# Four layers of a graph network on one core: row factors in smaller pieces, records gathered by fours, a ring of five PSUM banks

## The chip, the cores and the metric

The kernel runs on one core of a Trainium2 chip, as one program. A core has four compute engines with a queue each: PE (TensorE, with weight loads shown apart as PEld), DVE (VectorE), ACT (ScalarE) and POOL (GpSimd); SP issues DMAs. Matrices' sums are formed in PSUM, in 8 banks of 128 x 512 float32; all other data of the core lie in SBUF.[...] The metric is the device time of one launch in microseconds (us), as the median of several runs; the traces each hold one profiled execution.

## The reference

There are 8192 nodes with 32 features, `x`, and 262144 edges sorted by destination, so 32 a node in the mean. Four layers follow on each other; each adds its sum over the edges to x and normalizes the rows:

```python
edge_index = jnp.stack([src, dst])
x = _layernorm(x + _L0_gnn_ref(x, L0_gnn_weight, src, dst, edge_type_64), axis=-1)
x = _layernorm(x + _L1_gnn_ref(x, edge_index, edge_weight), axis=-1)
x = _layernorm(x + _L2_gnn_ref(x, edge_index), axis=-1)
x = _layernorm(x + _L3_gnn_ref(x, edge_index, edge_attr_4, edge_attr_32, L3_gnn_W1, ...), axis=-1)
```

Layer 0 multiplies `x[src]` with one of 64 matrices of 32 x 32, chosen by the edge's type, and sums over the edges of each destination. Layer 1 sums `x[src] * edge_weight`, layer 2 sums `x[src]`. Layer 3 makes for each edge a vector of 256 weights, `w = relu(ea32 @ W1 + b1) @ W2 + b2`, read as four 8 x 8 matrices, and combines them with the gathered row and the edge's four numbers `edge_sh`:

```python
m0 = ALPHA * (einsum('ei,eio->eo', s_e * sh0[:, None], w_000)
              + C110 * einsum('eim,em,eio->eo', v_e, sh1, w_110))
m1 = ALPHA * (einsum('ei,em,eio->eom', s_e, sh1, w_011)
              + einsum('eim,eio->eom', v_e * sh0[:, None, None], w_101))
```

where `s_e` are the first 8 features of `x[src]` and `v_e` the other 24 as 8 x 3. `m0` and `m1` are summed over each destination's edges, and a small product of x itself is added.

## The kernel before

Edges are worked in tiles of 128 (one edge per partition); 2048 tiles make 256 groups of 8. A sum over destinations is a matmul of a one-hot matrix (128 edges x 128 places of a moving window of nodes; `one_hot`, L505) with the tile's values; the groups' windows are brought together later by shifted matmuls (`windows`, L495). The order of the work is the order in which this code issues it to each engine's queue. `X.after(mark)` makes engine X wait for a mark, `X.mark(ins)` makes one. Helpers: `own` marks an operation and makes its engine wait for it, `now(X)` is X's newest mark, and a `Landing` counts the arrivals of DMAs. All indirect gathers (128 rows by 128 indices) are issued by POOL in one place, `indirect`, so they carry L383 in the profile.

**Table, from the start.** For every node and edge type the product is made once: 64 steps, each four matmuls (L404), two evictions of 128 x 1024 (L410) and one store of 1 MB into `ytab` (L412, by SP) from a ring of `NY` = 5 buffers. Beside it the generator `beginnings()` runs, one piece (up to the next `yield`) per step: it counts edges per node by one-hot matmuls (L321, L325, L326), takes prefix sums (from L346), then gathers 64 records of 768 bytes a partition (`begun["rec"]`), and checks. The 64 gathers are issued in one piece. While the generator has pieces left (`busy`), ACT makes both evictions of a step, afterwards ACT and DVE one each. The gathers of layer 0 wait for all stores of the table.

**Layer 0.** `slots` turns the gathered records about (PE transposes, ACT's evictions L537). Then for each group: eight row gathers from `ytab`, 12 groups ahead, in two halves by `fetch_rows`, where the first half waits for the mark of that group's aggregation on PE and the second for PE's newest mark; the split into three bf16 parts on DVE (`parts`, L619 to L624); the one-hot (L505); eight matmuls (L657) into bank 0 or 1, which change over every four groups; and, from group 8 on, `matrices`, which builds the adjacency matrices of layers 1 and 2 for the coming layers: one-hots on DVE (L557, L559, L562), then four units of eight matmuls each (L571) into one of two bank pairs, 3/4 and 5/6, two evictions by ACT of 128 x 512 a unit (L575, L576, one of each kind of matrix), and stores of 1 MB and 0.5 MB by SP (L580, L581). After every four groups `bank_out` reduces the aggregate bank, and eight times in the layer `windows` accumulates in bank 2 and `normalize` follows.

**Layers 1 and 2** load these matrices back and multiply (L730, L733).

**Layer 3.** First the z-stage adds the small product: 16 times a transpose (PE L852), an eviction (ACT L854), a matmul (PE L856) and an add on DVE. Then a loop over 512 quads of four tiles: `hidden` makes two quads' hidden vectors (PE L883, ACT L891); PE makes the 256 weights of four tiles (L907) in one of two bank pairs and marks `w`; `fetch_rows` issues the four gathers of the quad `AHEAD` = 12 further on, which wait for the `w` of the quad just made; PE aggregates the quad four back (L916), which waits for its `v`; DVE multiplies weights with factors (L944, L947, three L951), forms the one-hot (L505), and its mark `v` frees the weights' banks too. L931 and L936 end the quad before. The factors, products of the gathered row with `edge_sh`, are made for 32 tiles (8 quads) at once, two quads before they are needed: `factors`, L825 to L836.

Of the kernel before, what the change touches and what calls it, by code (L numbers as in the profile page):

```python
# [21 lines left out]
P = 128  # L22
# [123 lines left out]
def raw_layers(tc, x, a, w0, w1, b1, w2, si, m, bad):  # L146
# [34 lines left out]
    def now(f):  # L181
        return (f.sem, f.n)
# [100 lines left out]
    def beginnings():  # L283
# [72 lines left out]
        im = own(V, V.e.tensor_scalar(idx, idx, RG.bit_length() - 1, None, op0=OP.arith_shift_right))  # L356

        G.after(im)
        r_ld = Landing(tc, "ld_rec")
        for k in range(64):  # L360
            begun["rec"] = r_ld.add(indirect(rg[:, k].rearrange("p s f -> p (s f)"), a["rec"], idx[:, k:k + 1]))
# [4 lines left out]
        V.after(src_in, row_in)  # L366
        begun["row"] = own(V, V.e.scalar_tensor_tensor(row, src, float(R), row, op0=OP.mult, op1=OP.add))
# [173 lines left out]

    oh_used = [None, None]
    bank_free = [None, None]
# [4 lines left out]
    def matrices(i):  # L548

        b, pp, k0 = i % 2, i // 2, 16 * (i % 2)  # L550
        WB = 8
        if i % WB == 0:
            n = min(WB * 16, CB * 16 - i * 16)
            V.after(now(V))
            own(V, V.e.tensor_copy(w_ps[:, 0:n], meta_w.rearrange("p n k -> p (n k)")[:, i * 16:i * 16 + n]))
        V.after(oh_used[b])
        own(V, V.e.tensor_tensor(oh_k[:, b, :, 0, :], iota[:, None, 0:64].to_broadcast([P, 16, 64]),  # L557
                                 meta_k[:, pp, k0:k0 + 16, None].to_broadcast([P, 16, 64]), op=OP.is_equal))
        V.e.tensor_tensor(oh_l[:, b], iota[:, None, :].to_broadcast([P, 16, P]),  # L559
                          meta_l[:, pp, k0:k0 + 16, None].to_broadcast([P, 16, P]), op=OP.is_equal)  # L560
        wo = (i % WB) * 16
        vm = V.mark(V.e.tensor_tensor(oh_k[:, b, :, 1, :], oh_k[:, b, :, 0, :],  # L562
                                      w_ps[:, wo:wo + 16, None].to_broadcast([P, 16, 64]), op=OP.mult))
        PE.after(vm)
        for q in range(4):
            bk = 3 + 2 * (units[0] % 2)
            PE.after(bank_free[units[0] % 2])
            for j in range(4):
                for h in range(2):
                    hs_ = slice(64 * h, 64 * h + 64)  # L570
                    ins = PE.e.matmul(bank[:, bk + h, :].rearrange("p (c s j) -> p c s j", s=64, j=4)[:, :, :, j],  # L571
                                      oh_l[hs_, b, 4 * q + j, :], oh_k[hs_, b, 4 * q + j], start=True, stop=True)
            pm = PE.mark(ins)
            A.after(pm, st_ld[b].mark() if q == 0 and st_ld[b].n else None)
            A.e.activation(st_c[:, b, q], bank[:, bk:bk + 2, 0:256], AF.Copy)  # L575
            bank_free[units[0] % 2] = am = A.mark(A.e.activation(st_a[:, b, q], bank[:, bk:bk + 2, 256:512], AF.Copy))  # L576
            units[0] += 1
        oh_used[b] = pm
        S.after(am)
        st_ld[b].add(S.e.dma_start(amat[:, 2048 * i:2048 * (i + 1)], st_a[:, b].rearrange("p u h c -> p (u h c)")))  # L580
        st_ld[b].add(S.e.dma_start(cmat[:, 2048 * i:2048 * (i + 1)], st_c[:, b].rearrange("p u h c -> p (u h c)")))  # L581
# [6 lines left out]
    acc_free = [None]  # L588
# [50 lines left out]
    for g in range(GG + 2):  # L639
        if g >= 2 and (g - 2) % per == per - 1:  # L640
            vm = bank_out((g - 2) // per)
            while done < NB // LC and ready(done) <= g - 1:
                pm = windows(done, bank[:, 2, 0:LC * D], (acc_free[0], vm))
                acc_free[0] = normalize(0, done, bank[:, 2, 0:LC * D], pm, x_a, x_b)
# [119 lines left out]
    vs = cut(WT, 8, 3)  # L764
    a1 = cut(WT, 8)
# [42 lines left out]
    AHEAD = 12  # L808
    rows = {}

    def fetch_rows(q):

        if q < NQ:
            G.after(quad.get(q - AHEAD, {}).get("w"))
            rows[q // 8] = gathers(xtab, src, q // 8, q % 8 * 4, 4)

    def factors(s):

        k, landed = rows[s]
        b = batch[s]  # L820
        b["xg"] = k
        shv = sh[:, s % 3]
        u = s % 2
        V.after(b["s"])
        sm = V.mark(V.e.tensor_scalar(shv, shv, ALPHA, None, op0=OP.mult))  # L825
        V.after(*landed, sm)
        xv = xg[:, k]
        v = xv[:, :, 8:].rearrange("p t (i m) -> p t i m", m=3)
        vmk = V.mark(V.e.tensor_tensor(vs, v, shv[:, :, None, 1:4].to_broadcast([P, WT, 8, 3]), op=OP.mult))
        V.e.tensor_tensor(a0[:, u, :, 0:8], xv[:, :, 0:8], shv[:, :, 0:1].to_broadcast([P, WT, 8]), op=OP.mult)  # L830
        V.e.tensor_tensor(vm[:, u].rearrange("p t m i -> p t i m"), v,
                          shv[:, :, None, 0:1].to_broadcast([P, WT, 8, 3]), op=OP.mult)
# [3 lines left out]
        b["f"] = V.mark(V.e.tensor_scalar(a0[:, u, :, 8:16], a1, float(C110), None, op0=OP.mult))  # L836
# [62 lines left out]
    for q in range(NQ + LAG3 + 2):  # L899
# [21 lines left out]
        if q % 8 == 6 and q // 8 + 1 < NS:  # L921
            s = q // 8 + 1
            factors(s)
        V.after(prev)
        if q < NQ:
            V.after(batch[q // 8]["f"])
# [11 lines left out]
        if q < NQ:  # L938
# [3 lines left out]
            pq = p[:, q % NP]  # L942
            V.after(quad[q]["w"])
# [6 lines left out]
            for mm in range(3):  # L950
                V.e.tensor_tensor(pq[:, :, 128 + 64 * mm:192 + 64 * mm].rearrange("p t (o i) -> p t o i", i=8),  # L951
                                  wp[:, :, 192:256].rearrange("p t (o i) -> p t o i", i=8),
                                  vm[:, u, qs, mm, None, :].to_broadcast([P, 4, 8, 8]), op=OP.mult)
            ins = one_hot(oh[:, q % NO], 4 * q, 4)
# [501 lines left out]
```

## Time and profile before

| what | value |
|---|---|
| median of 3 runs | 7668.28 us (7660.74 to 7670.0) |
| the profiled execution | 7583.78 us |
| its span, first to last instruction | 7581.8 us |
| mean granted TensorE clock | 0.794 |
| table: to the first row gather of layer 0 | 271.4 us |
| layer 0: last row gather | 3432.6 us |
| layer 3: first row gather | 4522.6 us |
| HBM read, written | 521 MB, 472 MB |

The page's second part shows the stages by tenths of busy time in slices of 190 us (DMA is the busy share of the core's 16 DMA engines):

```profile
PE   5326665556555665654544867889989988888998
...
DVE  3336676677676767764000005666666667666676
...
POOL 3466565656566666650000016666666666666663
...
DMA  8416655556555555668999971111111111111111
```

The first slice and a half are the table, slices 2 to 18 mostly layer 0, 19 to 23 layers 1 and 2 (DMA at 6 to 9), the rest layer 3. In a row of a group or a timeline, "DMA_INDIRECT f_arena<-fytab,f_row" is a row gather of layer 0, `f_arena<-fxtab,f_src` one of layer 3; "remote" and "another core or an unknown queue" are waits for which the profile names no releaser. A wait for several semaphores is put down to the one that came last.

### The profile page before, as it was taken

The page shows a single profiled execution, that of the slowest core. Times are in us where ns is not written, and L with a number is a line of the kernel's source. Part 1 is how long each engine was busy: PE and PEld are TensorE (multiplying, and loading weights), DVE is VectorE, ACT ScalarE, POOL GpSimd, SP SyncE. Part 2 cuts the span into 40 slices and gives each one's busy share as a digit, 9 for nine tenths or more (in the row PEclk, how much of TensorE's full clock was granted, in tenths as well). Part 3 has the DMA queues.
Part 4 walks back from the last instruction along what each step waited for, and adds up shares of the span by engine and source line. Part 5 has one row for each costly group of instructions (what it writes and reads, how often), then busy time and mean ns, then how long its engine had stood idle before and what let it go on. Part 6 is the DMA issues. An engine that isn't in the chain of part 4 may idle for free.

```text
span 7581.8 us, 85791 instructions
## 1 busy us (share of the span) xinstructions
PE 5254.6 (69%) x34036; PEld 3717.5 (49%) x34036; DVE 4352.7 (57%) x8312; ACT 1629.6 (21%) x2812; POOL 3996.6 (53%) x4174
## 2 busy tenths in 40 slices
PE   5326665556555665654544867889989988888998
PEld 2115555555555555553222434555555555555555
DVE  3336676677676767764000005666666667666676
ACT  3213333333333333332000001111111111111111
POOL 3466565656566666650000016666666666666663
PEclk7557677777777777777777877999998999899989
DMA  8416655556555555668999971111111111111111
GB/s 285 149 36 145 144 150 139 145 144 152 145 145 145 144 151 138 152 142 279 428 431 428 386 289 18 28 23 25 24 24 24 24 24 24 24 24 24 25 24 20
DMA packets 290731, 999.29 MB, mean 132 GB/s; under 512 B 99021, under 2 KB 175886, under 8 KB 250638
## 3 DMA queue, kind: packets, MB, share of 16 engines
q1 hardware_dynamic: 155742, 916.89, 32.2%
q0 software_dynamic: 134144, 73.67, 12.2%
q8 instruction: 269, 4.41, 0.2%
q10 hardware_dynamic: 432, 3.15, 0.1%
q14 instruction: 144, 1.18, 0.1%
HBM read 521.39 MB, written 471.99 MB: 131 GB/s over the span
## 4 chain that ended last, share of the span: by engine, by line
PE 55%; another core or an unknown queue 11%; DMA 11%; issue 9%; DVE 8%; ACT 5%; POOL 0%; SPq 0%; DVEq 0%; ACTq 0%; POOLq 0%
PE bank L571 18%; PE bank L916 14%; PE bank L907 11%; DMA f_arena<-famat 7%; PE bank L657 3%; PE bank L883 3%; DMA f_arena<-fcmat 3%; ACT f_arena L576 3%; PE bank L730 2%; PE bank L733 2%; ACT f_arena L575 2%; DVE f_arena L951 1%; DVE f_arena L505 1%; PE bank L495 1%
## 5 line engine op out<-in xcount | busy, mean ns | idle before, releaser
L383 POOL DMA_INDIRECT f_arena<-fxtab,f_src x2048 | 1967.3, 961 | 2099.2 <-DVE f_arena L787 1089.0
L383 POOL DMA_INDIRECT f_arena<-fytab,f_row x2048 | 1962.0, 958 | 1280.5 <-issue 548.2
L571 PE MATMUL bank<-f_arena 64*128 64x128 f32 x16384 | 1566.7, 365 | 963.4 <-ACT f_arena L576 682.8
L571 PEld LDWEIGHTS bank<-f_arena 64*128 64x128 f32 x16384 | 1463.3, 272 | 1100.6 <-issue 938.7
L916 PE MATMUL bank<-f_arena 128*128 128x344 f32 x4096 | 1420.3, 489 | 65.4 <-issue 63.7
L907 PE MATMUL bank<-f_arena 65*128 65x256 f32 x4096 | 1075.3, 405 | 176.2 <-issue 161.0
L916 PEld LDWEIGHTS bank<-f_arena 128*128 128x128 f32 x4096 | 842.8, 207 | 509.3 <-issue 217.5
L907 PEld LDWEIGHTS bank<-f_arena 65*128 65x128 f32 x4096 | 785.2, 198 | 559.3 <-issue 361.0
L575 ACT ACTIVATE f_arena<-bank 128x512 bf16<-128x512 f32 x1024 | 613.0, 599 | 1925.4 <-PE bank L571 816.8
L891 ACT ACTIVATE f_arena<-bank,f_arena 64x512 f32<-64x512 f32 x512 | 351.3, 686 | 2500.1 <-remote 1001.6
L557 DVE TENSOR_TENSOR f_arena<-bank,f_arena 128x1024 f32<-128x1024 f32 x256 | 313.3, 1224 | 759.8 <-PE bank L657 440.4
L505 DVE TENSOR_TENSOR f_arena<-bank,f_rel 128x512 f32<-128x512 f32 (+1 forms) x768 | 660.9, 861 | 139.9 <-ACT f_arena L537 127.7
L944 DVE TENSOR_TENSOR f_arena<-bank,f_arena 128x256 f32<-128x256 f32 x512 | 214.7, 419 | 845.0 <-PE bank L907 324.4
L576 ACT ACTIVATE f_arena<-bank 128x512 f32<-128x512 f32 x1024 | 611.7, 597 | 0.0
L559 DVE TENSOR_TENSOR f_arena<-bank,f_arena 128x2048 f32<-128x2048 f32 x256 | 586.6, 2291 | 8.8
L951 DVE TENSOR_TENSOR f_arena<-bank,f_arena 128x256 f32<-128x256 f32 x1536 | 552.0, 416 | 0.0
L730 PE MATMUL bank<-f_arena,f_x_b 128*32 128x256 f32 x4096 | 293.2, 457 | 344.9 <-DMA f_arena<-famat 344.9
L657 PE MATMUL bank<-f_arena 128*128 128x96 bf16 x2048 | 216.7, 222 | 357.7 <-issue 215.5
L730 PEld LDWEIGHTS bank<-f_arena,f_x_b 128*32 128x32 f32 x4096 | 145.1, 131 | 481.8 <-DMA f_arena<-famat 318.0
L454 DVE TENSOR_TENSOR f_lnf<-bank,f_x_b 128x256 f32<-128x256 f32 x8 | 3.4, 425 | 615.0 <-PE bank L710 615.0
L947 DVE TENSOR_TENSOR f_arena<-bank,f_arena 128x512 f32<-128x512 f32 x512 | 348.8, 681 | 0.0
L657 PEld LDWEIGHTS bank<-f_arena 128*128 128x128 bf16 x2048 | 122.0, 104 | 404.5 <-issue 260.2
(133 smaller groups left out, 3532.6 us busy)
## 6 DMA issues: line engine op xcount, KB each, us to landing
famat<-f_arena SPq DMA_DIRECT2D x256, 1024.0 KB
fcmat<-f_arena SPq DMA_DIRECT2D x256, 512.0 KB
fytab<-f_arena SPq DMA_DIRECT2D x64, 1024.0 KB
f_arena<-fytab,f_row POOLq DMA_INDIRECT x2048
f_arena<-fxtab,f_src POOLq DMA_INDIRECT x2048
f_arena<-laid_ea SPq DMA_DIRECT2D x64, 512.0 KB
f_arena<-laid_ea SPq DMA_DIRECT2D x64, 64.0 KB
f_arena<-laid_xT ACTq DMA_DIRECT2D x1, 1024.0 KB, 8.9
```

What stands on the lines that cost most here:

```text
L383: return G.e.indirect_dma_start(out=dest, out_offset=None, in_=table, in_offset=bass.IndirectOffsetOnAxis(ap=ix, axis=0))
L505: return V.e.tensor_tensor(o, iota[:, None, :].to_broadcast([P, n, P]), rel[:, t:t + n, None].to_broadcast([P, n, P]), op=OP.is_equal)
L559: V.e.tensor_tensor(oh_l[:, b], iota[:, None, :].to_broadcast([P, 16, P]), meta_l[:, pp, k0:k0 + 16, None].to_broadcast([P, 16, P]), op=OP ...
L571: ins = PE.e.matmul(bank[:, bk + h, :].rearrange("p (c s j) -> p c s j", s=64, j=4)[:, :, :, j], oh_l[hs_, b, 4 * q + j, :], oh_k[hs_, b, ...
L575: A.e.activation(st_c[:, b, q], bank[:, bk:bk + 2, 0:256], AF.Copy)
L576: bank_free[units[0] % 2] = am = A.mark(A.e.activation(st_a[:, b, q], bank[:, bk:bk + 2, 256:512], AF.Copy))
L657: ins = PE.e.matmul(bank[:, bk, 3 * c * D:3 * (c + 1) * D], oh[:, h, t, :], xp[:, g % 4, t].rearrange("p c f -> p (c f)"), start=(t == 0), ...
L730: ins = PE.e.matmul(bank[q * D:(q + 1) * D, b, 0:256].rearrange("p (u h j) -> p u h j", h=2, j=4), x_b[:, s, :], mv[:, s], start=(s < 4), ...
L891: quad[q + h] = dict(h=A.mark(A.e.activation(hs[0:64, (q + h) % 4], bank[64 * h:64 * h + 64, 2, :], AF.Relu, bias=b1_s[64 * h:64 * h + 64])))
L907: ins = PE.e.matmul(wp[:, t, :], hs[0:65, q % 4, t * P:(t + 1) * P], w2_s[0:65], start=True, stop=True)
L916: ins = PE.e.matmul(bank[:, g % 2, 0:MW], oh[:, c % NO, t, :], p[:, c % NP, t, :], start=(c % 2 == 0 and t == 0), stop=(c % 2 == 1 and t = ...
L951: V.e.tensor_tensor(pq[:, :, 128 + 64 * mm:192 + 64 * mm].rearrange("p t (o i) -> p t o i", i=8), wp[:, :, 192:256].rearrange("p t (o i) - ...
```

## The change

Three edits in one step, and two moves of single operations on DVE.

- **Records by fours.** After each four of the 64 record gathers the generator gives way twice to the table's steps (once from the 48th on), and POOL waits for PE's newest mark before it goes on. The 64 gathers take 26 further pieces, so `busy` holds until step 60 of 64 in place of 34. The operation that makes `row` (L367) goes ahead of the gathers.
- **Ring of five banks.** The units of `matrices` take the banks 2 to 6 in turn, two a unit; each half of a unit is evicted by itself, so there are four evictions of 128 x 256 a unit, and each bank is given back by itself. A unit's first matmul waits for its two banks. Bank 2 is now in the ring, so the windows of layer 0 are accumulated in the aggregate bank that `bank_out` has just reduced, and that bank is free after `normalize` has read it.
- **Factors by 8 tiles.** `factors(r)` makes the factors of 8 tiles, the two quads after the present two, every second quad; only the scaling of `edge_sh` (L825) stays at 32 tiles. The scratch tiles `vs` and `a1` are cut to 8 tiles, so each call waits for the last one. `AHEAD` of layer 3 goes from 12 to 8.
- **One-hot first.** In a quad of layer 3 the one-hot stands ahead of the wait for `w`, and the last of the three L951 bears the mark `v`.

```diff
@@ -354,17 +354,21 @@
         own(V, V.e.tensor_scalar(idx, pre[:, 1 - f, :], small[:, 7:8], None, op0=OP.add))
         own(V, V.e.tensor_scalar(idx2, idx, RG - 1, None, op0=OP.bitwise_and))
         im = own(V, V.e.tensor_scalar(idx, idx, RG.bit_length() - 1, None, op0=OP.arith_shift_right))
+        V.after(src_in, row_in)
+        begun["row"] = own(V, V.e.scalar_tensor_tensor(row, src, float(R), row, op0=OP.mult, op1=OP.add))
 
         G.after(im)
         r_ld = Landing(tc, "ld_rec")
         for k in range(64):
+            if k % 4 == 0 and k:
+                for _ in range(2 if k < 48 else 1):
+                    yield
+                G.after(now(PE))
             begun["rec"] = r_ld.add(indirect(rg[:, k].rearrange("p s f -> p (s f)"), a["rec"], idx[:, k:k + 1]))
         yield
 
         own(V, V.e.tensor_tensor(pre[:, f, :], idx2, deg, op=OP.add))
         own(V, V.e.tensor_reduce(ok[:, 3:4], pre[:, f, :], AX.X, OP.max))
-        V.after(src_in, row_in)
-        begun["row"] = own(V, V.e.scalar_tensor_tensor(row, src, float(R), row, op0=OP.mult, op1=OP.add))
         V.e.tensor_reduce(ok[:, 0:1], rel, AX.X, OP.max)
         own(V, V.e.tensor_reduce(ok[:, 1:2], rel, AX.X, OP.min))
         own(V, V.e.tensor_scalar(ok[:, 0:1], ok[:, 0:1], float(P - 1), None, op0=OP.is_gt))
@@ -539,8 +543,9 @@
         return now(A)
 
 
+    acc_free = [None]
     oh_used = [None, None]
-    bank_free = [None, None]
+    bank_free = {k: (acc_free[0] if k == 2 else None) for k in range(2, 7)}
     st_ld = [Landing(tc, f"st_m{k}") for k in range(2)]
     w_up = [None]
     units = [0]
@@ -563,17 +568,18 @@
                                       w_ps[:, wo:wo + 16, None].to_broadcast([P, 16, 64]), op=OP.mult))
         PE.after(vm)
         for q in range(4):
-            bk = 3 + 2 * (units[0] % 2)
-            PE.after(bank_free[units[0] % 2])
+            bk = [2 + (2 * units[0] + h) % 5 for h in range(2)]
+            PE.after(*(bank_free[b5] for b5 in bk))
             for j in range(4):
                 for h in range(2):
                     hs_ = slice(64 * h, 64 * h + 64)
-                    ins = PE.e.matmul(bank[:, bk + h, :].rearrange("p (c s j) -> p c s j", s=64, j=4)[:, :, :, j],
+                    ins = PE.e.matmul(bank[:, bk[h], :].rearrange("p (c s j) -> p c s j", s=64, j=4)[:, :, :, j],
                                       oh_l[hs_, b, 4 * q + j, :], oh_k[hs_, b, 4 * q + j], start=True, stop=True)
             pm = PE.mark(ins)
             A.after(pm, st_ld[b].mark() if q == 0 and st_ld[b].n else None)
-            A.e.activation(st_c[:, b, q], bank[:, bk:bk + 2, 0:256], AF.Copy)
-            bank_free[units[0] % 2] = am = A.mark(A.e.activation(st_a[:, b, q], bank[:, bk:bk + 2, 256:512], AF.Copy))
+            for h in range(2):
+                A.e.activation(st_c[:, b, q, h], bank[:, bk[h], 0:256], AF.Copy)
+                bank_free[bk[h]] = am = A.mark(A.e.activation(st_a[:, b, q, h], bank[:, bk[h], 256:512], AF.Copy))
             units[0] += 1
         oh_used[b] = pm
         S.after(am)
@@ -585,7 +591,6 @@
     NO = 4
     oh_free = [None] * NO
     agg_free = [freed[0], freed[0]]
-    acc_free = [None]
     G.after(r0, *y_done)
     V.after(*y_done)
     PE.after(*freed)
@@ -640,8 +645,8 @@
         if g >= 2 and (g - 2) % per == per - 1:
             vm = bank_out((g - 2) // per)
             while done < NB // LC and ready(done) <= g - 1:
-                pm = windows(done, bank[:, 2, 0:LC * D], (acc_free[0], vm))
-                acc_free[0] = normalize(0, done, bank[:, 2, 0:LC * D], pm, x_a, x_b)
+                acc = bank[:, (g - 2) // per % 2, 0:LC * D]
+                agg_free[(g - 2) // per % 2] = vm = normalize(0, done, acc, windows(done, acc, (vm,)), x_a, x_b)
                 done += 1
         if g >= GG:
             continue
@@ -761,8 +766,8 @@
     ef = cut(3, 2, 512)
     sh = cut(3, WT, 4)
     a0 = cut(2, WT, 16)
-    vs = cut(WT, 8, 3)
-    a1 = cut(WT, 8)
+    vs = cut(8, 8, 3)
+    a1 = cut(8, 8)
     vm = cut(2, WT, 3, 8)
     MW = 344
     NP, NO = 6, 6
@@ -805,35 +810,39 @@
                                          a["ea4"][:, 4 * s * WT:4 * (s + 1) * WT]))
         batch[s] = dict(e=e_in, s=s_in)
 
-    AHEAD = 12
+    AHEAD = 8
     rows = {}
+    factor = {}
 
     def fetch_rows(q):
 
         if q < NQ:
             G.after(quad.get(q - AHEAD, {}).get("w"))
-            rows[q // 8] = gathers(xtab, src, q // 8, q % 8 * 4, 4)
-
-    def factors(s):
-
-        k, landed = rows[s]
+            rows[q // 2] = gathers(xtab, src, q // 8, q % 8 * 4, 4)
+
+    def factors(r):
+
+        k, landed = rows[r]
+        s, ts = r // 4, slice(r % 4 * 8, r % 4 * 8 + 8)
         b = batch[s]
         b["xg"] = k
-        shv = sh[:, s % 3]
         u = s % 2
-        V.after(b["s"])
-        sm = V.mark(V.e.tensor_scalar(shv, shv, ALPHA, None, op0=OP.mult))
-        V.after(*landed, sm)
-        xv = xg[:, k]
+        if r % 4 == 0:
+            shb = sh[:, s % 3]
+            V.after(b["s"])
+            V.after(V.mark(V.e.tensor_scalar(shb, shb, ALPHA, None, op0=OP.mult)))
+        shv = sh[:, s % 3, ts]
+        V.after(landed[-1], factor.get(r - 1))
+        xv = xg[:, k, ts]
         v = xv[:, :, 8:].rearrange("p t (i m) -> p t i m", m=3)
-        vmk = V.mark(V.e.tensor_tensor(vs, v, shv[:, :, None, 1:4].to_broadcast([P, WT, 8, 3]), op=OP.mult))
-        V.e.tensor_tensor(a0[:, u, :, 0:8], xv[:, :, 0:8], shv[:, :, 0:1].to_broadcast([P, WT, 8]), op=OP.mult)
-        V.e.tensor_tensor(vm[:, u].rearrange("p t m i -> p t i m"), v,
-                          shv[:, :, None, 0:1].to_broadcast([P, WT, 8, 3]), op=OP.mult)
+        vmk = V.mark(V.e.tensor_tensor(vs, v, shv[:, :, None, 1:4].to_broadcast([P, 8, 8, 3]), op=OP.mult))
+        V.e.tensor_tensor(a0[:, u, ts, 0:8], xv[:, :, 0:8], shv[:, :, 0:1].to_broadcast([P, 8, 8]), op=OP.mult)
+        V.e.tensor_tensor(vm[:, u, ts].rearrange("p t m i -> p t i m"), v,
+                          shv[:, :, None, 0:1].to_broadcast([P, 8, 8, 3]), op=OP.mult)
         V.after(vmk)
         rm = V.mark(V.e.tensor_reduce(a1, vs, AX.X, OP.add))
         V.after(rm)
-        b["f"] = V.mark(V.e.tensor_scalar(a0[:, u, :, 8:16], a1, float(C110), None, op0=OP.mult))
+        factor[r] = V.mark(V.e.tensor_scalar(a0[:, u, ts, 8:16], a1, float(C110), None, op0=OP.mult))
 
 
     V.after(c_in)
@@ -918,12 +927,11 @@
             quad[c]["a"] = PE.mark(ins)
 
         prev = (V.sem, V.n)
-        if q % 8 == 6 and q // 8 + 1 < NS:
-            s = q // 8 + 1
-            factors(s)
+        if q % 2 == 0 and q + 2 < NQ:
+            factors(q // 2 + 1)
         V.after(prev)
         if q < NQ:
-            V.after(batch[q // 8]["f"])
+            V.after(factor[q // 2])
         V.after(quad.get(q - NP, {}).get("a"))
         ins = None
         if 0 <= q - 2 < NQ:
@@ -940,6 +948,7 @@
             s, u = q // 8, (q // 8) % 2
             qs = slice((q % 8) * 4, (q % 8) * 4 + 4)
             pq = p[:, q % NP]
+            one_hot(oh[:, q % NO], 4 * q, 4)
             V.after(quad[q]["w"])
             V.e.tensor_tensor(pr[:, q % 2].rearrange("p t (o i) -> p t o i", i=8),
                               wp[:, :, 128:192].rearrange("p t (o i) -> p t o i", i=8),
@@ -948,10 +957,9 @@
                               wp[:, :, 0:128].rearrange("p t (o k) -> p t o k", k=16),
                               a0[:, u, qs, None, :].to_broadcast([P, 4, 8, 16]), op=OP.mult)
             for mm in range(3):
-                V.e.tensor_tensor(pq[:, :, 128 + 64 * mm:192 + 64 * mm].rearrange("p t (o i) -> p t o i", i=8),
-                                  wp[:, :, 192:256].rearrange("p t (o i) -> p t o i", i=8),
+                ins = V.e.tensor_tensor(pq[:, :, 128 + 64 * mm:192 + 64 * mm].rearrange("p t (o i) -> p t o i", i=8),
+                                        wp[:, :, 192:256].rearrange("p t (o i) -> p t o i", i=8),
                                   vm[:, u, qs, mm, None, :].to_broadcast([P, 4, 8, 8]), op=OP.mult)
-            ins = one_hot(oh[:, q % NO], 4 * q, 4)
         if ins is not None:
             d = V.mark(ins)
             if q < NQ + 2:
```

## The prediction

> **What bounds the kernel now.** I read the page's busy line first, then windows of each stage, then the order of time on the engine that each stage waits for.
>
> ```profile
> PE 5254.6 (69%) x34036; PEld 3717.5 (49%) x34036; DVE 4352.7 (57%) x8312; ACT 1629.6 (21%) x2812; POOL 3996.6 (53%) x4174
> ```
>
> No engine is full over the span, so each stage has its own limit. The windows (columns: busy us and instructions of PE, PEld, DVE, ACT, POOL; granted clock; DMA share; GB/s), two from the table, one of layer 0, one of layer 3's start, one of layer 3:
>
> ```profile
> 150.00:200.00 50.00, 10.38 (x20) 2.52 (x20) 2.45 (x2) 3.07 (x3) 31.24 (x33) 0.50 0.36 109
> 200.00:250.00 50.00, 42.47 (x156) 15.05 (x156) 24.48 (x21) 20.34 (x20) 0.00 (x0) 0.64 0.97 358
> 1000.00:2000.00 1000.00, 593.15 (x6130) 530.59 (x6126) 687.05 (x867) 362.59 (x686) 614.51 (x650) 0.73 0.58 145
> 4530.00:4590.00 60.00, 14.34 (x43) 8.75 (x45) 4.47 (x16) 3.76 (x14) 39.72 (x42) 0.50 0.14 29
> 5000.00:6000.00 1000.00, 901.98 (x3145) 577.57 (x3146) 689.14 (x1789) 121.36 (x180) 654.70 (x687) 0.91 0.13 24
> ```
>
> The table stage runs at 358 GB/s, which is the stores of ytab, except where POOL gathers the records: there PE does 20 matmuls in 50 us. Its chain shows waits that end at no known releaser, and ACT's timeline shows evictions only every 20 us:
>
> ```profile
> 152.24 22.36 another core or an unknown queue
> 174.64 21.65 another core or an unknown queue
> ```
> ```profile
> 152.22 1.02 ACT L410 ACTIVATE f_arena<-bank 128x1024 f32<-128x1024 f32 x1 [17.17 <-remote]
> 174.62 1.02 ACT L410 ACTIVATE f_arena<-bank 128x1024 f32<-128x1024 f32 x1 [21.38 <-remote]
> 196.32 1.02 ACT L410 ACTIVATE f_arena<-bank 128x1024 f32<-128x1024 f32 x1 [20.68 <-remote]
> ```
>
> DVE does its evictions midway between these, so the two step every 11 us, and both come unstuck when POOL's 64 gathers end at 191. The same pattern sits in layers 0 and 3: while POOL issues one indirect gather after another (0.95 us and 0.30 us of issue, 1.25 us each), PE's completion signals reach the other engines late, and all that are outstanding arrive together about 1.7 us after POOL stops. In layer 0 (POOL's timeline, then the timeline of all engines; start, length, engine, line, and in brackets the idle time before and its releaser):
>
> ```profile
> 1211.59 0.95 POOL L383 DMA_INDIRECT f_arena<-fytab,f_row  x1 [0.31 <-issue]
> 1214.66 0.95 POOL L383 DMA_INDIRECT f_arena<-fytab,f_row  x1 [2.12 <-PE bank L657]
> ```
> ```profile
> 1214.26 0.60 ACT L575 ACTIVATE f_arena<-bank 128x512 bf16<-128x512 f32 x1 [4.64 <-PE bank L657]
> 1214.42 1.22 DVE L557 TENSOR_TENSOR f_arena<-bank,f_arena 128x1024 f32<-128x1024 f32 x1 [3.64 <-PE bank L657]
> 1214.66 0.95 POOL L383 DMA_INDIRECT f_arena<-fytab,f_row  x1 [2.12 <-PE bank L657]
> 1215.49 2.90 PE L571 MATMUL bank<-f_arena 64*128 64x128 f32 x23 [2.39 <-ACT f_arena L576]
> ```
>
> ACT, DVE and POOL all go on within 0.4 us, 1.7 us after POOL's last gather ended at 1212.54; PE follows when ACT has emptied a bank pair. That the gathers delay the signals is an inference; no engine's record names it. Between 560 and 3430 POOL pauses 240 times, and in 226 of them the first PE signal comes 1.5 to 1.8 us after POOL's end; the period is 8 gathers x 1.25 + 1.76 = 11.76 us a group. Layer 3 has 157 such pauses in 4700:7500, median 2.47 us, and 2048 x 1.25 + 391 us of pauses = 2951 us, its length from 4595 to 7547. So layers 0 and 3 are paced by POOL's gathers and these pauses; in layers 1 and 2 (431 GB/s) the change touches nothing.
>
> [...] gathers and stores add up in one DMA share, yet at 0.36 the engines were not what held the table.[...] L951 takes 0.416 us for 256 elements, L829 0.960 us for 768.
>
> **Part 1, records by fours.** Before: PE has done 30 of 64 steps at 110 us and 42 at 200; the table ends at 271 (first row gather 271.4). After: four gathers, then POOL waits for PE's newest mark and for two table steps (one from k = 48). Four gathers take 5.0 us, two steps issue about 32 matmuls and two signals each; in layer 0 the first 64 or more PE records after a pause still signalled promptly, so I expect few late ones. Then the stores are the limit: 1 MB at 358 GB/s is 2.93 us, 34 steps 99.6 us; the gathers' own traffic, at 0.36 us of the 16 engines each (an estimate from the 0.36 share in that window, in which a gather takes 1.25 us and few stores run: at most 0.45), 64 x 0.36 = 23 us. From 112.7 (start of the record phase): 112.7 + 99.6 + 23 + 4 (checks, last landing) = 239. With all of the gathers' traffic beneath the stores 216. With every four costing POOL's cycle (5.0 + 2.1 = 7.1 us for two steps) 251. If steps stand as before during each four, 295. The evictions fall to ACT (`busy` holds till step 60): 2 x 0.93 = 1.9 us a step, under 2.93, so hidden; if ACT waited for stores' buffers anyway nothing changes. Queued behind POOL's new wait are only more record gathers and, at the end, layer 0's row gathers, which wait for the table anyway. L367 moved ahead is one DVE operation in DVE's idle time: nothing. I take 231, between 216 and 239: 271 - 231 = **-40**; ends -55 and +24.
>
> **Part 2, ring of five banks.** ACT's evictions go from two of 128x512 (0.60 us) to four of 128x256 a unit.[...] PE may restart after half a pair, about 0.7 us after the flush in place of 1.1 to 1.2: 0.45 us earlier. But POOL's next pause begins when its eight gathers are out, and it ends 1.65 us after that whatever PE did in between; its second fetch waits for the matrices' last mark, which PE reaches long before the gathers are out and which only arrives late. So the period stays 11.76 and the ring is worth **0**. If all 0.45 carried to each of the 240 pauses: -108.[...] Layer 0's eight windows, now accumulated in the aggregate bank just drained, start at the same mark as before; that bank is wanted again three groups (35 us) later: nothing.
>
> **Part 3, layer 3.** The factor operations cost 0.96 + 0.42 + 1.50 + 0.93 + 0.30 = 4.1 us for 32 tiles, 64 times = 262 us. For 8 tiles: 0.36 (L829 at 192 elements[...]) + 0.2 + 0.4 + 0.3 + 0.2 = 1.5 us, 256 times = 384 us, so DVE gains 122 us of work. DVE is 69% busy here and has 829 us of idle before L944, waiting for w: hidden, and 122 if that cover is gone. One_hot (0.68 us) goes ahead of the same wait: its time falls into idle, v's mark comes 0.68 us earlier after w. Steady rate: POOL is held by its lead on w, 10 to 12 quads now, 8 then; a shorter lead moves every gather by the same number of quads and leaves the rate at 5.0 + pauses. So 0, with ends -130 (half of the bursts of 4.1 us was on the path) and +160 (lead of 8 gives one more 2.5 us pause in each of 64 batches).
>
> At the start the lead counts. Gathers run 4522.6 to 4582.3 (48 of them), and slow the 16 transposes of the z-stage to 8.4 us each against 1.38 before:
>
> ```profile
> 4561.21 0.28 ACT L854 ACTIVATE f_arena<-bank 128x128 f32<-128x128 f32 x1 [8.12 <-issue]
> 4569.61 0.28 ACT L854 ACTIVATE f_arena<-bank 128x128 f32<-128x128 f32 x1 [8.12 <-remote]
> 4578.70 0.28 ACT L854 ACTIVATE f_arena<-bank 128x128 f32<-128x128 f32 x1 [8.82 <-remote]
> 4586.41 0.28 ACT L854 ACTIVATE f_arena<-bank 128x128 f32<-128x128 f32 x1 [7.42 <-remote]
> ```
>
> With 32 gathers POOL stops at 4562.5; the last three then follow at 1.4 to 2.8 us instead of 8: the stage ends near 4574 in place of 4589.5, -15; and at the end of the layer the eight last quads run without gathers instead of twelve, 4 x (5.78 - 4.65) = +4.5. Net **-11**.
>
> **Sum.** -40 + 0 + 0 - 11 = -51. Against the profiled execution 7583.8 (span 7581.8, 2 us around it) that is 7533; the median of the runs shown, 7668.3, is 84 us longer than the profiled one, so for it 7668 - 51 = **7617**.
>
> **Rivals.**
>
> Ring pays (0.2): PE has 631 us of waits on L576, which speaks for it; the fixed 1.65 us after POOL's end speaks against. 7617 - 108 = 7509.
>
> Bursts in layer 3 were on the path (0.1): PE is 90% busy there, so little room, but ACT L891 waits for PE 2000 us. 7617 - 130 = 7487.
>
> Pacing gains nothing (0.08): stores or steps stand during each four. 7668 - 11 = 7657, within 0.2%.
>
> Slower (0.12): layer 3's added DVE work. After each flush DVE has several quads' products in its queue[...]. It decides once 66 of the 122 us land on the path, since 51 + 15 must be made up to pass +0.2%; wholly, 7617 + 122 = 7739. (The extra pauses of part 3 would give 7617 + 160 = 7777, beyond the range.)
>
> The forecast itself (0.5).
>
> **Chances and range.** About 0.2%, 15 us, is what this measurement can tell from no change. Faster: 0.5 + 0.2 + 0.1 = 0.8, of which a little sits in the same band, and a little of the pacing case reaches faster: 0.8. Same 0.08, slower 0.12. The likeliest case's own range, from part 1's ends -55 and -19 and ±15 elsewhere, is 7590 to 7650. Two in ten may lie outside: leaving out most of slower and part of the bursts' case gives 7500 to 7680.
>
> **What would show it.** The first row gather of layer 0 at 216 to 251 and over 300 GB/s from 110 on (part 1; wrong if it still comes at 271). Layer 0's period 11.76 and POOL's gap near 2.1 (ring worth nothing; wrong if the gap or period falls by 0.4). Layer 3's first L907 some 15 us sooner after layer 2, its quad 5.78 us, L831 near 0.4 us x256, idle before L944 smaller by about 120 (part 3; wrong if the quad's period moves by over 0.1, which is 51 us). The largest danger is that the delayed signals follow another rule than POOL's pauses, for instance the count of outstanding signals: then the ring and the lead of 8 change layers 0 and 3 by far more than I count.

## The result, and the profile after

The changed kernel takes 7601.5 us (median of 4 runs, 7595.8 to 7605.0) against 7664.5 for the kernel before (7659.4 to 7670.0): ratio 0.992, interval 0.9905 to 0.9934, 63 us less. Forecast were 7617 and 51 us less.

The two profiled executions say the opposite: a span of 7603.1 after, 7581.8 before. The first trace of before is an execution 84 us under its median, so it can't be set against the trace of after. The kernel before was therefore run again beside three variants, and its second trace (span 7631.8) is the one compared below.

The windows of the changed kernel (columns as in the prediction's fence), two of the table's, one of layer 0, one of layer 3:

```profile
110.00:150.00 40.00, 30.59 (x110) 10.85 (x107) 8.70 (x13) 24.18 (x25) 27.66 (x27) 0.67 0.90 331
150.00:200.00 50.00, 36.53 (x110) 11.60 (x112) 0.00 (x0) 26.24 (x27) 32.79 (x35) 0.64 1.02 379
1000.00:2000.00 1000.00, 632.27 (x5972) 559.98 (x5974) 670.61 (x847) 394.79 (x1332) 604.93 (x640) 0.66 0.54 142
5000.00:6000.00 1000.00, 910.04 (x3125) 587.83 (x3124) 697.04 (x2083) 119.49 (x178) 644.35 (x680) 0.90 0.12 24
```

Between 150 and 200 us POOL still issues 35 gathers, but PE now does 110 matmuls in place of 20, and the DMA engines, which carry the stores and the gathers, are full (1.02, 379 GB/s against 0.36, 109). In layer 0 ACT has twice the instructions, as the ring asks, and PE's granted clock is lower, 0.66 against 0.73; layer 3 hardly differs from before. ACT's timeline at the end of the z-stage:

```profile
4569.25 0.28 ACT L863 ACTIVATE f_arena<-bank 128x128 f32<-128x128 f32 x1 [7.42 <-remote]
4574.18 0.28 ACT L863 ACTIVATE f_arena<-bank 128x128 f32<-128x128 f32 x1 [4.65 <-remote]
4575.55 0.28 ACT L863 ACTIVATE f_arena<-bank 128x128 f32<-128x128 f32 x1 [1.10 <-PE bank L861]
4576.93 0.28 ACT L863 ACTIVATE f_arena<-bank 128x128 f32<-128x128 f32 x1 [1.10 <-PE bank L861]
4578.31 0.28 ACT L863 ACTIVATE f_arena<-bank 128x128 f32<-128x128 f32 x1 [1.10 <-PE bank L861]
```

Five to eight us a step while POOL gathers, 1.38 us once it has stopped. Where the time went, by stages read from the first and last gathers and weight matmuls of each trace (us; the last three columns are the experiments below):

| stage | before, second trace | after | records alone | ring alone | layer 3 alone |
|---|---|---|---|---|---|
| table, to the first row gather | 272.0 | 230.1 | 228.1 | 272.8 | 271.5 |
| layer 0, first to last row gather | 3199.0 | 3220.9 | 3198.8 | 3219.4 | 3203.0 |
| layers 1 and 2, to layer 3's first gather | 1076.8 | 1078.7 | 1075.2 | 1075.6 | 1072.7 |
| from there to the first weights' matmul | 73.9 | 55.6 | 75.3 | 73.4 | 54.9 |
| first to last weights' matmul | 2977.7 | 2985.3 | 2983.1 | 2981.7 | 2978.7 |
| span | 7631.8 | 7603.1 | 7593.0 | 7655.1 | 7613.3 |

The traced execution of before lies 8 us under the median of its runs, the other four within 4 us of theirs. So against the timed medians the table makes gains look up to some 10 us smaller, and losses larger.

### The profile page after: what moved, and what is told of

It reads as the page before. It is cut to its first block, busy times and chain, and to the rows that moved or that the text cites. A ratio compares the mean times of both kernels' runs of the same rounds, so it can differ in the third digit from the quotient of the medians.

```text
span 7603.1 us, 89477 instructions
## 1 busy us (share of the span) xinstructions
PE 5438.7 (72%) x34036; PEld 3862.9 (51%) x34036; DVE 4371.1 (57%) x9246; ACT 1780.5 (23%) x4886; POOL 3972.1 (52%) x4174
## 4 chain that ended last, share of the span: by engine, by line
PE 42%; another core or an unknown queue 17%; DVE 15%; DMA 10%; ACT 10%; issue 5%; POOL 0%; SPq 0%; DVEq 0%; ACTq 0%; POOLq 0%
PE bank L576 12%; PE bank L925 12%; PE bank L916 10%; DMA f_arena<-famat 6%; ACT f_arena L582 4%; ACT f_arena L581 4%; DVE f_arena L960 3%; DMA f_arena<-fcmat 3%; PE bank L892 2%; DVE f_arena L956 2%; PE bank L735 2%; DVE f_arena L509 2%; PE bank L738 2%; PE bank L408 1%
## 5 line engine op out<-in xcount | busy, mean ns | idle before, releaser
L387 POOL DMA_INDIRECT f_arena<-fxtab,f_src x2048 | 1943.0, 949 | 2145.1 <-DVE f_arena L792 1077.8
L576 PE MATMUL bank<-f_arena 64*128 64x128 f32 x16384 | 1632.3, 375 | 894.7 <-ACT f_arena L582 560.0
L576 PEld LDWEIGHTS bank<-f_arena 64*128 64x128 f32 x16384 | 1525.4, 281 | 989.3 <-ACT f_arena L582 472.7
L916 PE MATMUL bank<-f_arena 65*128 65x256 f32 x4096 | 1111.0, 418 | 196.0 <-DVE f_arena L960 193.6
L581 ACT ACTIVATE f_arena<-bank 128x256 bf16<-128x256 f32 x2048 | 817.8, 399 | 1849.1 <-remote 1100.2
L916 PEld LDWEIGHTS bank<-f_arena 65*128 65x128 f32 x4096 | 809.3, 204 | 593.9 <-DVE f_arena L960 295.5
L925 PEld LDWEIGHTS bank<-f_arena 128*128 128x128 f32 x4096 | 861.8, 211 | 436.6 <-issue 138.1
L582 ACT ACTIVATE f_arena<-bank 128x256 f32<-128x256 f32 x2048 | 828.8, 405 | 0.0
L662 PE MATMUL bank<-f_arena 128*128 128x96 bf16 x2048 | 271.8, 261 | 349.9 <-issue 209.7
L662 PEld LDWEIGHTS bank<-f_arena 128*128 128x128 bf16 x2048 | 150.0, 120 | 468.6 <-issue 337.4
```

The lines of the kernel that those rows point to most:

```text
L387: return G.e.indirect_dma_start(out=dest, out_offset=None, in_=table, in_offset=bass.IndirectOffsetOnAxis(ap=ix, axis=0))
L576: ins = PE.e.matmul(bank[:, bk[h], :].rearrange("p (c s j) -> p c s j", s=64, j=4)[:, :, :, j], oh_l[hs_, b, 4 * q + j, :], oh_k[hs_, b, 4 ...
L581: A.e.activation(st_c[:, b, q, h], bank[:, bk[h], 0:256], AF.Copy)
L582: bank_free[bk[h]] = am = A.mark(A.e.activation(st_a[:, b, q, h], bank[:, bk[h], 256:512], AF.Copy))
L662: ins = PE.e.matmul(bank[:, bk, 3 * c * D:3 * (c + 1) * D], oh[:, h, t, :], xp[:, g % 4, t].rearrange("p c f -> p (c f)"), start=(t == 0), ...
L916: ins = PE.e.matmul(wp[:, t, :], hs[0:65, q % 4, t * P:(t + 1) * P], w2_s[0:65], start=True, stop=True)
```

## The experiments

**First group: each part alone**, with the kernel before, on one chip where before takes 7645.0 us.

The kernel before, unchanged.

> The kernel before once more, unchanged, for a trace from the same chip as the next three. Theory (pauses of POOL set layers 0 and 3): 1.000 of before; the length of layer 0 (first to last row gather) is about 50 us over the 3161 us of the first trace of before, because the pause after eight gathers is about 1.85 us here, as in the changed kernel's trace, in place of 1.65; 240 x 0.2 = 48. Rival (the ring makes layer 0 slower): 3161 us again and pauses of 1.65.

Measured 7641.8, ratio 0.9996 (0.9989 to 1.0002). Layer 0 took 3199.0 us, the median time from POOL's end to PE's first signal was 1.79 us and the whole pause 2.22; in the first trace of before they were 1.65 and 2.07. So 38 of the 60 us by which layer 0 seemed to have grown were there without the change. Forecast were about 50. The length of the pause varies between executions or chips; why isn't known.

Records by fours alone (with the move of the operation that makes `row`, which is left out here):

```diff
+            if k % 4 == 0 and k:
+                for _ in range(2 if k < 48 else 1):
+                    yield
+                G.after(now(PE))
```

> Before with the records by fours alone. Theory: table ends about 230 in place of 271, all else as before: 41 us less, ratio 0.9946. Rival (the pacing moves work to later): under 20 us less.

Measured 7593.8, ratio 0.993 (0.9914 to 0.9947): 51 us less. The trace has the table's end at 228.1, 44 us sooner, and all other stages within 6 us. The window from 150 to 200 us, first in the second trace of before, then in this one:

```profile
150.00:200.00 50.00, 10.39 (x20) 2.51 (x20) 3.67 (x3) 2.05 (x2) 31.01 (x33) 0.50 0.41 130
150.00:200.00 50.00, 33.48 (x108) 11.52 (x110) 0.00 (x0) 27.17 (x29) 31.77 (x34) 0.64 0.99 369
```

POOL issues 34 gathers in place of 33, and beside them PE does 108 matmuls in place of 20. POOL does not pause after every four: it goes on at once or within about 0.5 us at most of them and stops only four times for more than 1 us, for 2.5 to 3.9 us, so that its last gather ends at 202.9 us in place of 190.8. In before the longest wait of a unit, from the modelled end of its matmuls to its eviction, is 30.4 us, here 12.5. Theory kept: the timed interval, 41 to 66 us less, holds both the forecast and the trace's 44.

The ring of five banks alone (its hunks of the diff):

> Before with the ring of five banks alone. Theory: the period of layer 0 is that of eight gathers and a pause, so nothing: within 15 us. Rival A (PE's earlier restart carries): about 108 us less. Rival B (four evictions of 0.40 us in place of two of 0.60 us lengthen ACT's path, 0.4 us a unit): 40 us more or worse.

Measured 7656.8, ratio 1.0015 (1.0008 to 1.0022): 12 us slower, and in the trace layer 0 is 20 us longer. "Nothing" is not quite right, rival A is refuted, and rival B's 40 us is too much. First a single group. PE's timeline over it, first of before and then of the ring (start, length of the run of matmuls, idle time before it and its releaser):

```profile
1198.81 4.78 PE L571 MATMUL bank<-f_arena 64*128 64x128 f32 x48 [1.00 <-ACT f_arena L576]
1204.84 1.16 PE L571 MATMUL bank<-f_arena 64*128 64x128 f32 x16 [1.26 <-issue]
```
```profile
1201.56 5.32 PE L572 MATMUL bank<-f_arena 64*128 64x128 f32 x48 [0.43 <-ACT f_arena L578]
1209.10 1.29 PE L572 MATMUL bank<-f_arena 64*128 64x128 f32 x16 [2.21 <-issue]
```

In both, PE runs three units (x48) and then waits for the fourth's banks. The fourth unit starts 7.5 us after the first in the ring, in place of 6.0, since ACT gets the second unit's signal later. ACT's timelines, again before and ring:

```profile
1197.58 0.60 ACT L575 ACTIVATE f_arena<-bank 128x512 bf16<-128x512 f32 x1 [3.27 <-remote]
...
1203.70 0.60 ACT L575 ACTIVATE f_arena<-bank 128x512 bf16<-128x512 f32 x1 [1.70 <-PE bank L571]
```
```profile
1200.76 0.38 ACT L577 ACTIVATE f_arena<-bank 128x256 bf16<-128x256 f32 x1 [3.87 <-remote]
...
1208.30 0.38 ACT L577 ACTIVATE f_arena<-bank 128x256 bf16<-128x256 f32 x1 [3.41 <-PE bank L572]
```

After the pause PE starts 1.23 us behind ACT's first eviction in before (1197.58 to 1198.81) and 0.80 us behind it in the ring (1200.76 to 1201.56): the 0.45 us of the forecast, the author's estimate, are there (0.43). But the second unit's matmuls end at 1202.6 in before and at 1205.35 in the ring (modelled ends); ACT starts on it 1.1 us later in the one and 2.9 in the other. So the gain is lost again within the group.

This is not where the 20 us lie, though. POOL makes 244 pauses in layer 0. The 190 of them away from the layer's window sums add up to 515 to 519 us in all five traces of the table, with the ring or without. The 54 around the seven window sums that fall among the gathers (from 25 us before each to 60 us after it) add up to 175, 175 and 180 us in the three traces with the layer 0 of before, and to 194 and 192 in the two with the ring. POOL's pauses around one of these sums, in before and in the ring:

```profile
1684.19 0.94 POOL L383 DMA_INDIRECT f_arena<-fytab,f_row  x1 [3.62 <-PE bank L657]
...
1693.83 0.94 POOL L383 DMA_INDIRECT f_arena<-fytab,f_row  x1 [4.94 <-PE bank L571]
...
1708.03 0.95 POOL L383 DMA_INDIRECT f_arena<-fytab,f_row  x1 [4.52 <-PE bank L571]
```
```profile
1689.91 0.94 POOL L383 DMA_INDIRECT f_arena<-fytab,f_row  x1 [4.51 <-PE bank L658]
...
1699.75 0.95 POOL L383 DMA_INDIRECT f_arena<-fytab,f_row  x1 [5.15 <-PE bank L572]
...
1714.34 0.95 POOL L383 DMA_INDIRECT f_arena<-fytab,f_row  x1 [4.89 <-PE bank L572]
```

The matmuls of the seven sums (L495), each from its first start to its last end, take 27 to 28 us together in the three traces and 33 to 34 in the two. The edit touches these sums twice: they moved to another bank, and the units ahead of them on PE changed. No run separates the two. There is a further rival that no run tests: with the ring PE is granted a lower clock in this layer, 0.65 and 0.66 between 1000 and 2000 us against 0.71 in the other three traces. Whether that is a cause of the loss or goes with it is open.

Layer 3's part alone (its hunks of the diff):

> Before with layer 3's part alone (factors by 8 tiles, lead of 8, one-hot first). Theory: 17 us less at the start of the layer (32 gathers in place of 48 beside the z-stage), 4 us more at its end, the quad's period unchanged: 13 us less. Rival A (DVE's bursts were on the path): 60 us less or better. Rival B (DVE's added work or the shorter lead costs): 20 us more or worse, with more POOL pauses than in the trace of before.

Measured 7619.3, ratio 0.9967 (0.9955 to 0.998): 26 us less by medians. The start is 54.9 in place of 73.9 us, 19 less; the main part 2978.7 against 2977.7. Theory kept for the start and the main part; the timed interval, 15 to 34 us less, holds the 19 of the start and lies just above the forecast of 13. The factors' operations, L825 to L836, went from 276 to 422 us of DVE in these traces (L831 from 1.498 to 0.485 us, four times as often), and the idle time before L944 only from 868 to 821: the added work is hidden, though most of it not in that wait.

**Second and third group.** These two fell on two other chips, on both of which the kernel before takes 6481 us. There PE's signals are not late: in layer 0 POOL makes no pause of over 1 us in any trace. The kernel before itself was not traced there; the runs without POOL's wait, below, have its layers 0 and 3. Ratios of these groups stand for such a chip alone.

Without the ring, in both groups (layer 0's lines as before, the rest as after):

> The changed kernel with layer 0's two bank pairs put back: records by fours and layer 3's part alone. Theory (the three parts add up: -51 and -25 by their own runs, the ring costs): about 76 us under before, ratio 0.990, layer 0 as long as in before (3199 us on this chip's trace). Rival (the ring pays once the table is shorter): no faster than the changed kernel, 0.992.

> The changed kernel with layer 0's two bank pairs put back. Theory: where signals are late, 12 to 20 us faster than the changed kernel (ratio 0.990), layer 0 shorter by about 20 us; where they are not, equal to it within 5 us. Rival (the ring pays beside the other two parts): slower than the changed kernel.

Measured 6435.4, 0.9931 (0.9915 to 0.9948), and 6431.5, 0.9919 (0.9903 to 0.9936). The first expectation doesn't fit this chip: layer 0 is 2580 us long, 2048 gathers at 1.26.

By fours, but without POOL's wait, in both groups:

```diff
-                G.after(now(PE))
```

> Before with the records by fours, but without POOL's wait for PE between them: the gathers are issued back to back as before, the generator still gives way, and ACT still makes both evictions to step 60. Theory (POOL's pauses let PE's signals through): the table ends at about 271 as in before, no gain; if it ends later than 271, ACT alone is slower when signals are late. Rival (the order of the generator or the evictions by ACT made the gain): the table ends near 230, about 45 us less.

> Before with the records by fours, but without POOL's wait for PE between them. Theory (POOL's pauses let PE's signals through): where signals are late, the table ends at about 271 or later and nothing is gained, against 228 with the wait. Rival (the generator's order or ACT's evictions made the gain): the table ends near 230 there too. Where signals are not late: 224, no gain, as measured.

Measured 6481.1, ratio 0.9999 (0.999 to 1.0008), and 6479.9, 0.9999 (the same interval). The table ends at 224.1 and 224.0 us: the gathers go out back to back, and the steps run beside them as they should. ACT's timeline there, in the middle of the gathers:

```profile
152.69 1.94 ACT L413 ACTIVATE f_arena<-bank 128x1024 f32<-128x1024 f32 x2 [1.37 <-DMA fytab<-f_arena]
155.80 1.94 ACT L413 ACTIVATE f_arena<-bank 128x1024 f32<-128x1024 f32 x2 [1.18 <-DMA fytab<-f_arena]
```

A step every 3.1 us, waiting for the stores. With the wait the table ends at 223.5 to 225.3, the same. So on such a chip the first part is worth nothing, and these runs can't say which of its ingredients, wait, order or ACT's evictions, makes the gain where signals are late.

Layer 3's lead back at 12, without the ring:

```diff
-    AHEAD = 8
+    AHEAD = 12
```

> Records by fours and layer 3's part, two bank pairs, with layer 3's lead back at 12 quads. Theory (the lead is what shortens the start): from the layer's first gather to its first L907 73 us in place of 55, the main part of the layer within 10 us, so 15 us slower than the same with a lead of 8. Rival (small factors shorten the start or the main part): no slower.

Measured 6436.9, ratio 0.9931 (0.9915 to 0.9948), equal to a lead of 8 (6435.4). The start takes 32.8 and 32.2 us. Nothing is late here that 16 more gathers could hold up, so the lead's part stays untested where it counts. The main part is another matter: 2552.9 us with 12, 2551.8 with 8, but 2593.6 with before's layer 3 in the same group. The small factors, or the one-hot put first, gain 42 us here, and the lead has no share in it; no run has one of the two without the other. DVE's timeline in the run without the wait in the third group, whose layer 3 is that of before, and then that of the changed kernel:

```profile
5033.86 0.22 DVE L828 TENSOR_SCALAR f_arena<-f_arena 128x128 f32<-128x128 f32 x1
5039.73 0.97 DVE L832 TENSOR_TENSOR f_arena<-f_arena 128x768 f32<-128x768 f32 x1 [5.66 <-DMA f_arena<-fxtab,f_src]
...
5040.97 1.54 DVE L834 TENSOR_TENSOR f_arena<-f_arena 128x768 f32<-128x768 f32 x1
```
```profile
5000.64 0.36 DVE L838 TENSOR_TENSOR f_arena<-f_arena 128x192 f32<-128x192 f32 x1 [1.89 <-DMA f_arena<-fxtab,f_src]
...
5001.05 0.49 DVE L840 TENSOR_TENSOR f_arena<-f_arena 128x192 f32<-128x192 f32 x1
```

In before DVE stands for the last of 32 tiles' gathers, here 5.7 us, and then works off 4.1 us at a stretch. POOL pauses seven times in that layer, for 0.8 to 2.5 us, which is 13 us beyond the pitch in all. In the changed kernel there is no such pause, and 2048 gathers take 2569 us, 1.25 each: POOL is the bound.

Most of the gain lies at the layer's end. From the last gather to the last weights' matmul it takes 43 and 45 us with the factors of before (second and third group) and 13 to 16 us with the small ones, with a lead of 12 as with 8; the stretch of the gathers itself is only 12 and 27 us shorter. A batch can't begin before its last row has come. So in before POOL stands 9 to 12 quads ahead of PE throughout the layer, with the small factors 3 to 6, and PE has to work off this distance when the gathers are over.

The changed kernel in the third group:

> The changed kernel once more, beside the next three on one chip. Theory: on a chip where before takes about 7650 us and PE's signals are late beside gathers, 0.992 as first measured. On a chip where before takes 6481 us and no signals are late: table and layer 3's start gain nothing, layer 3's main part 42 us, layer 0 is POOL's gathers back to back, so the ring is worth nothing: 0.993, equal to the kernel without the ring.

Measured 6433.1, ratio 0.9926 (0.9909 to 0.9943). Layer 3's main part is 2550.1 us against 2607.9 with before's layer 3, layer 0 2580.0 against 2585.1 without the ring. The two traced executions set against it lie 15 and 9 us over the medians of their runs, so the 58 us are too many and the 5 us say nothing. By medians the small factors and the one-hot are worth 44 to 48 us on these chips, as against the runs without the wait.

Two bank pairs, four evictions, in both groups:

```diff
+            for h in range(2):
+                A.e.activation(st_c[:, b, q, h], bank[:, bk + h, 0:256], AF.Copy)
+                bank_free[units[0] % 2] = am = A.mark(A.e.activation(st_a[:, b, q, h], bank[:, bk + h, 256:512], AF.Copy))
```

> Records by fours and layer 3's part, two bank pairs, but four evictions of 128x256 a unit as in the ring. Theory (the ring costs because PE runs a unit further ahead before the signal that it then waits for): as without the ring, within 10 us. Rival (ACT's longer evictions are the cost): 12 to 20 us slower than without the ring, layer 0 near 3219 us.

> The changed kernel with two bank pairs in layer 0, but four evictions of 128x256 a unit as in the ring. Theory (the ring costs because PE runs a unit further ahead before the signal that it then waits for): within 5 us of the kernel with two bank pairs and two evictions. Rival (the smaller evictions are the cost): 12 to 20 us slower than that one, layer 0 longer by 20 us.

Measured 6436.5, 0.9929 (0.9913 to 0.9946), and 6431.9, 0.9921 (0.9904 to 0.9937): equal to two evictions and to the ring. POOL's gathers bound layer 0 there (no pause of over 1 us in any trace, and 2580 us for the 2048 with two evictions as with the ring), so this can't part the two readings of the ring's 12 us.

## Why the prediction was right, step by step

- **What bounds the kernel.** Right for a chip with late signals: 1.25 us a gather plus one pause a group. The time from POOL's end to the first signal, 1.65 us, was taken as fixed; it is 1.79 in the second trace of before and 1.84 in the changed kernel's. On the other chips the same gathers bring no pause of over 1 us in layer 0, 2048 of them in 2580 us.
- **Records by fours, -40.** Right: -44 in the trace of this part alone, and the table ends at 228.1 there and at 230.1 in the changed kernel, against 231. The 231 was picked between 216 and 239 without a reason given for the place between them. In the trace of this part alone the DMA engines are full during the gathers (0.99, 369 GB/s between 150 and 200 us), which bears out that the stores are the limit. That pauses let the signals through fits the shorter waits in that trace, at most 12.5 us in place of 30.4, but it is argued: the run without pauses could not be tried where signals are late.
- **Ring, 0.** Mis-sized: +12 us timed, +20 in the trace. The term at fault is the one for the eight windows, which was put at "nothing" because they start at the same mark and their bank is wanted three groups later: 12 to 19 us of added pauses lie around them, and none elsewhere. The step that the matrices' last mark is reached "long before the gathers are out" doesn't hold with the ring either: in most groups its last matmul ends about 1.7 us before POOL's last gather without the ring and within half a us of that gather's end with it. But the pauses away from the windows grew by less than 4 us in all. ACT's own time hardly grew: a unit's four evictions take 0.40 us each and the two of before 0.60, but they overlap, and from the first start to the last end a unit takes 1.2 us in place of 1.1. Why the pauses around the windows are longer is open.
- **Layer 3's start, -15, and its end, +4.** The start was -19 in the part alone. The end took 45.5 us from the last gather to the last weights' matmul before and 27.2 in the part alone, so four quads at 4.6 us; with gathers beside them a quad takes 5.86, which makes +5. The added DVE work was 146 us in place of 122 and was hidden, as forecast. The 1.5 us for 8 tiles was the author's estimate; in the trace of the part alone the five operations take 0.35 + 0.22 + 0.49 + 0.33 + 0.20 = 1.6 us, so 32 tiles in four pieces take 6.3 us in place of 4.1.
- **Layer 3's steady rate, 0.** Right where signals are late (+1 us in the trace). On the other chips the factors' size does count, 44 to 48 us, about a third of what the bursts rival said, but mostly through the distance that is left at the layer's end and not through DVE's bursts of 4.1 us. On the chip with late signals POOL stands 10 to 12 quads ahead of PE with the lead of 12 and 6 to 8 with the lead of 8, so there the lead sets this distance. That this hid what the small factors gain is a reading; no run with late signals has them with the lead of 12.
- **The sum.** -51 against -63. The parts by their own runs, -51 +12 -26 = -65, add up to it. Two misses of like size, the ring's +12 and layer 3's -15 beyond its -11, nearly cancel; that is luck, and what is left is about the 11 us by which the records were timed better than forecast. The sum was rightly set against the median and not against the profiled execution, 84 us under it: the changed kernel's profiled execution is 3 us over its median. On the other chips the ratio is 0.993, nearly the same, but there the table and the start of layer 3 gain nothing and the small factors, or the one-hot, nearly all. That the two ratios agree is chance.
- **Rivals.** "Ring pays" fell; "pacing gains nothing" fell where signals are late and holds where they are not; "slower by DVE's work" fell.

The version without the ring should be some 12 us faster where signals are late, by the first group's sum, and is level elsewhere; it was not run on a chip of the first kind.

## What to carry to other kernels

Where a trace shows the other engines standing beside a long run of indirect gathers, try letting the run wait now and then for the others: here four stops of 2.5 to 3.9 us among 64 gathers went with 44 us less, and on the chips where nobody stood the table ended at the same time with the wait (223.5 to 225.3 us) as without it (224.0 and 224.1). Try making each piece of a batched step wait for no more than its own rows: here, on the chips without late signals, 13 to 16 us were left from the last gather to the last weights' matmul in place of 43 and 45, though the factors' work on DVE rose from 276 to 422 us (in the first group's traces), and the one-hot put first may have a share in it. More PSUM banks gained nothing in any run here, 12 us slower alone and level on the other chips, though PE had 631 us of waits for banks in layer 0. And take the trace of before from the same chip as the trace of after: before alone took 7645 us on one chip and 6481 on two others.

## What was not expected of the hardware

The kernel before took 7645 us on one chip and 6481 on two others, a difference of 15% that dwarfs the change. Nearly all of it lies beside POOL's gathers: layer 0 3199 against 2580 us, layer 3's main part 2978 against 2594 to 2608, the table 272 against 224 (in the run without POOL's wait); the stretch with layers 1 and 2, which has no gathers, differs by 65 to 67 of 1077 us. On the slower chip the other engines take up PE's results late while gathers run, which the author reads as late signals: between 150 and 200 us of the second trace of before PE does 20 matmuls and ACT and DVE five evictions, beside 33 gathers. In the third group's run without the wait, beside 34, PE does 124 and ACT 32. PE's granted clock differs as well, 0.71 against 0.82 between 1000 and 2000 us, and whether as a cause or because PE waits more is not known. What else differs between the chips no trace shows. Since the same gathers run on all these chips, they can be one condition of the lateness but not all of it.
